# A four-layer graph network on one core: exponentials three calls behind their subtractions, four copies on another engine, a later transpose, an earlier load

## The chip, the core and the metric

The kernel runs on one core of one Trainium2 chip. The metric is the time of one execution on the device in microseconds (us). The time before is the median of three runs, 2242.59 us (2240.81 to 2247.57). The profile comes from one execution that took 2241.24 us.

## The reference, cut to what matters

There are N = 2708 nodes with 512 features each and a sparse symmetric 0/1 matrix `adj`. Four layers follow each other, and the result of each goes through a residual sum and a layer norm:

```python
# layer 0
pooled = a_norm @ x + x;  y = relu(pooled @ W + b)
# layer 1
dis = (deg + EPS) ** -0.5
y = (dis[:, None] * adj * dis[None, :]) @ x @ W.T + b
# layer 2: two attention layers, one behind the other
Wh, Ws = jnp.split(x @ W, 2, axis=-1)
a = softmax(Wh @ Ws.T, axis=-1) * adj
x = leaky_relu(a @ Wh + x)
# layer 3: 8 heads
y = adj @ (H @ W) + b
# behind each layer
x = layernorm(x + y)
```

## The kernel before, in words

**Tiling.** The nodes make 22 row blocks, 21 of 128 rows and one of 20 (`NB` = 22). Columns are cut into six chunks (`CH`): four of 512, one of 384, one of 276. `Fast.run` does layers 0 and 1 in steps of one chunk and one group of row blocks, then the two attention layers, then layer 3. The wrapper class `Ordered` ties each instruction to the one issued before it on its engine, so every engine runs its instructions in exactly the order in which the program issues them. This has two consequences for a reader: the order in the Python code is the order on the chip, engine by engine, and an instruction that waits holds all that stand behind it on its engine. All instructions of the trace carry the line of that wrapper, L71; they are told apart by the names of their tiles.

**Layers 0 and 1.** A product `acc` is the sum over row blocks of a mask `m` (a byte tile `at`, cast by ScalarE) times x, which is split in two parts: `xh` (ScalarE) and `xl`, the rest (VectorE), both from `halve`. In layer 1 both are scaled with `dis`. The last block of 20 rows is handled by `fold`: it lays four quarters of its x, 32 rows each, under each other (four copies on ScalarE), and in layer 1 does the same with the 32 values of `dis` (tile `dis_f`, four copies on VectorE). VectorE also does the reductions `feeds`, from which the lists of neighbours are made.

**An attention layer.** For each chunk, PE computes the 22 score tiles `s` (products `sp`, `spx`, `spy`; chunks 0 and 1, `SEVEN`, by a scheme with seven products in place of eight). VectorE keeps the greatest score of each column (`top`). Two steps of PE bring it into the form that is subtracted: `shift_rows` (transposes `tr_top`, reductions, copies to `wide`) and `shift_columns` (transposes `tr_mx`, a ScalarE copy to `shift`). Then the chunk is softened, one row tile after the other. A call v of `soften` issues

- the subtraction of tile v on VectorE (`s<-s,shift`),
- the exponential of the tile that is `apart` calls behind on ScalarE (`s<-s`),
- another `apart` calls behind: the sum (`sum<-sum,s`) and the mask product (`s<-s,a`) on VectorE, and the store of the tile by SyncE's queue, SP (`pairs<-s`).

`apart` is 2 for the chunks of `SEVEN` and 1 for the others. So a chunk of `SEVEN` takes 26 calls, the others 24; behind the last tile's mask product `softened` is set to `SOFT`, the sign that the chunk may be gathered. Then GpSimd (POOL) gathers rows of the stored tiles by lists of neighbours (`g<-pairs,givers`, `fetch`), at most 10 outstanding, and PE weighs them (`acc<-g`, `weigh`). The end of a block goes to `xr` and `r`, by `y<-r` to memory and turned round to the next layer's `xt` (layer 0), or through the layer norm into `made`, the x of layer 3 (layer 1).

**The order around the change.** The planner keeps a clock of its own, `self.clock`: each group of matmuls moves it on by its planned time (512 columns: 4 x 512 / 2400 us). `later` and `pending` hold work that is due at a time of this clock; `until(clock, fill)` issues weighing steps, or where none is ready steps of `fill`, till the clock is reached. In `layer`, a chunk's 22 score steps carry the softening of the chunk before: behind step 4 the old chunk is put on the list, and from step 5 on each step calls `soften_next` once or twice in turn (always twice where two chunks wait). That is 26 calls from step 5 to 21. Behind the last chunk's scores comes the tail:

```python
        self.until(self.clock + 3, fill)
        self.shift_rows(last)
        self.until(self.clock + 3, fill)
        self.shift_columns(last)

        while chunks[-3].to_fetch:
            if not self.weigh() and not next(fill, False):
                assert self.weigh(True)
        done = self.clock + (2 if ly.number == 0 else 4)
        while last.softened < SOFT:
            self.soften(last)
            done += 1.4
            self.until(done, fill)
```

The `fill` of attention layer 0 is `second`, the projection of attention layer 1: the product of the two weight halves (`mix`, four steps, each ended by a ScalarE copy to `mixed`), loads of the weights and of chunk 0's x (`load_xt`: four DMAs of SP, 1 MB for a full chunk, `xt<-t`), sums of quarters for the seven products (`t1x` to `t4x`, `s1mixed` to `s4w`, on VectorE: `sum_xt`, `sum_sides`), and for each chunk `project_steps`: products `wst` (ScalarE copies to `wst_sb`), products `z` and stores of `z_sb` (`pairs<-z_sb`). The x of chunk k + 1 is loaded ahead of the products of chunk k. The `fill` of attention layer 1 is `early`, the first twelve parts of layer 3's products, of four steps with eight matmuls each; its parts t = 0 and 1 call `need`, which forces the weighing of row blocks up to 11 and up to 15, whether their gathers have landed or not.

The functions that the diff touches, and what calls them:

Of the kernel before, what the change touches and what calls it, by code (L numbers as in the profile page):

```python
# [22 lines left out]
NB = 22  # L23
# [4 lines left out]
CH = [(0, 512), (512, 512), (1024, 512), (1536, 512), (2048, 384), (2432, 276)]  # L28
# [8 lines left out]
QUARTERS, QW = 4, P // 4  # L37
# [16 lines left out]
class Ordered:  # L54


    def __init__(self, tc):
        self.tc, self.last = tc, {}
        for name in ("tensor", "vector", "scalar", "gpsimd", "sync"):
            setattr(self, name, OrderedEngine(self, getattr(tc.nc, name)))  # L60
# [440 lines left out]
}  # L501
STREAMED = 4
FIRST_LANDS = 16
SOFT = NB + 2 * 2
ALONE = 18
SEVEN = [0, 1]
PROJECTED = [0, 1]
# [44 lines left out]
class Fast:  # L552
# [275 lines left out]
    def fold(self, ly, x, s):  # L828


        nc = self.nc
        f = self.page(f"fold{ly.number}")[:, :P]
        for d in range(DC):
            nc.scalar.copy(f[d * QW : (d + 1) * QW], x[:QW, bass.ts(d, P)])
        if ly.number == 1:
            t = self.small.tile([P, 1], FP, tag="dis_f", name="dis_f")
            for d in range(DC):
                nc.vector.tensor_copy(t[d * QW : (d + 1) * QW], s[:QW])
            s = t
        return f, s  # L840

# [741 lines left out]
class Chunk:  # L1583


    def __init__(self, ly, k):
        self.ly, self.k, self.cw = ly, k, CH[k][1]
        self.name = f"{ly.number}_{k}"
        self.blocks = blocks_of(k)
        self.s, self.masks, self.ends = {}, {}, []  # L1590
        self.half = self.cw // 2
        self.seven = k in SEVEN
        self.part, self.complete, self.ready, self.top = {}, [], [], None
        self.softened = 0
        self.masks_ahead = 2 if k < STREAMED else 5
        self.apart = 2 if self.seven else 1
        self.fetched, self.rden = [], None
        self.x, self.first = {}, {}
        self.rows = set()
        self.mv = None  # L1600

        self.to_weigh = []
        for q, (i, _, _) in enumerate(self.blocks):
            ts = lists_of(i)
            self.to_weigh += [(q, t, t is ts[0], t is ts[-1]) for t in ts]
        self.to_fetch = [(q, t) for q, ts, _, _ in self.to_weigh for t in ts]
        self.first_fetch = self.to_fetch[0]
# [11 lines left out]
class Attention:  # L1619
# [656 lines left out]
    def soften_next(self):  # L2276


        if self.to_soften:
            self.soften(self.to_soften[0])  # L2280
            if self.to_soften[0].softened == SOFT:
                self.to_soften.pop(0)

    def soften(self, ch):


        nc, v, cw = self.nc, ch.softened, ch.cw
        ch.softened += 1
        if v < NB:
            n = rows_of(v)  # L2290
            s = ch.s[v][:n, :cw]
            nc.vector.tensor_sub(s, s, ch.shift[:n, :cw])
        j = v - ch.apart
        if 0 <= j < NB:
            s = ch.s[j][: rows_of(j), :cw]
            nc.scalar.activation(s, s, AF.Exp)
        j -= ch.apart
        if j < 0:
            return
        if j == NB - 1:  # L2300
            ch.softened = SOFT
        if j == 0 and ch.k >= 2:
            while self.chunks[ch.k - 2].to_fetch:
                self.weigh(True)
        if j % DC == 0 and j + ch.masks_ahead * DC < NB:
            self.load_mask(ch, j // DC + ch.masks_ahead)
        n = rows_of(j)
        s = ch.s[j][:n, :cw]
        if j == 0:
            ch.sum = self.page(f"sum{ch.name}")  # L2310
            nc.vector.tensor_copy(ch.sum[:, :cw], s)
        else:
            nc.vector.tensor_add(ch.sum[:n, :cw], ch.sum[:n, :cw], s)
        nc.vector.tensor_mul(s, s, ch.masks.pop(j)[:n, :cw])
        to = ch.ly.pairs[ch.k % 2][j * P : j * P + n, :]
        if cw == BANK:
            nc.sync.dma_start(
                to[:, : 2 * PAIR].rearrange("j (r x) -> j r x", x=PAIR)[:, :, D:],
                ch.s[j][:n, :].rearrange("j (r x) -> j r x", x=2 * P),
            )  # L2320
            return
        for r in range(2):
            w = min(2 * P, cw - r * 2 * P)
            nc.sync.dma_start(
                to[:, r * PAIR + D : r * PAIR + D + w],
                ch.s[j][:n, r * 2 * P : r * 2 * P + w],
            )
# [50 lines left out]
    def fetch_ahead(self):  # L2378
        count = sum(len(c.fetched) for c in self.chunks)
        for c in self.chunks:  # L2380
            while c.to_fetch:
                if c.softened < SOFT or count >= self.AHEAD:
                    return
# [140 lines left out]
    def layer(self, ly, chunks, fill):  # L2524
        f = self.f
        self.chunks, self.made = chunks, {}
        for k, ch in enumerate(chunks):
            old = chunks[k - 1] if k else None
            following = chunks[k + 1] if k + 1 < len(chunks) else None

            n = -1
            for what in self.walk(ch):
                if what == "mid":
                    self.soften_next()
                    self.weigh()
                    continue
                n += 1
                if old and n < old.masks_ahead:
                    self.load_mask(old, n)
                if not following and n > NB - 1 - ch.masks_ahead:  # L2540
                    self.load_mask(ch, n - NB + ch.masks_ahead)
                if old and n < 2:
                    self.greatest(old, last=n == 1)
                many = 2 if len(self.to_soften) > 1 else 1 + n % 2
                for _ in range(0 if ch.seven else many):
                    self.soften_next()
                f.beat()
                if n == 14 and k:
                    f.packed(k - 1)
                if following and n == 15:  # L2550
                    self.load_moving(following)
                if following and following.seven and n == 18:
                    self.sum_moving(following)
                if not following and n in (5, 11, 19):
                    next(fill)
                if ch.seven and not following.seven and n >= 7 and n % 4 == 3:
                    self.restore(ly, n // 4 - 1)
                if not ch.seven and n == 1:
                    for i in sorted(ly.sums):
                        self.restore(ly, i)  # L2560
                self.greatest(ch)

                for _ in range(3):
                    if not self.weigh():
                        break
                if old and n == 2:
                    self.shift_rows(old)
                if old and n == 4:
                    self.shift_columns(old)
                    self.to_soften.append(old)  # L2570
        assert not self.to_soften
        last = chunks[-1]
        self.greatest(last, last=True)
        self.until(self.clock + 3, fill)
        self.shift_rows(last)
        self.until(self.clock + 3, fill)
        self.shift_columns(last)
# [9 lines that stand above are left out]
        while any(c.to_weigh for c in chunks):  # L2587
            if not self.weigh() and not next(fill, False):
                assert self.weigh(True)
        while self.pending:  # L2590
            if not next(fill, False):
                self.pending.pop(0)[1]()
        for _ in fill:
            pass
# [13 lines left out]
    def second(self, first):  # L2608

        ly = self.layers[1]  # L2610
        mixing = self.mix(1)
        next(mixing)
        yield True
        self.load_w(ly)
        yield True
        self.load_xt(ly, 0)
        yield True
        yield from mixing
        if ly.seven:
            self.sum_xt(ly, 0)  # L2620
            yield from self.sum_sides(ly)
        for k in range(len(CH)):
            if k + 1 == len(CH) - 1:
                while self.pending:
                    self.pending.pop(0)[1]()
                self.first_moving(first)
            if k + 1 < len(CH):
                self.load_xt(ly, k + 1)
            yield from self.project_steps(ly, k)


# [63 lines left out]
```

## Time and profile before

| | before |
|---|---|
| median of three runs | 2242.59 us (2240.81 to 2247.57) |
| the profiled execution | 2241.24 us |
| its span, first to last instruction | 2239.3 us |
| mean granted clock of TensorE | 0.993 |
| PE idle in the span | 36.4 us |
| ScalarE's wait for VectorE's subtractions (`s` for `s`) | 53.7 us in 44 waits, longest 7.9 |
| gathers by POOL | 510, mean 1051 ns |
| moved by DMA | 502.29 MB, mean 224 GB/s |

How to read it: a row of a timeline gives start, duration, engine, operation, output from inputs, and, in brackets, how long the engine stood idle before it and what released it. A table of waits gives, for one engine, total us, number of waits and the longest. A table of windows gives for each stretch its length, the busy time of each engine (and its instructions), the granted clock (1.00 is full speed), the DMA engines' share and the rate. PE is TensorE's matmul, PEld its weight load, DVE VectorE, ACT ScalarE, SP the queue of SyncE. A DMA share over 1.00 means that all 16 engines had something to move all the time.

### The profile page before, as it was taken

To read this page: it belongs to the slowest core of one execution; us is meant where nothing else is said; L and a number is where in the kernel's file an instruction comes from. 1 tells how busy PE (TensorE), PEld (TensorE's weight loads), DVE (VectorE), ACT (ScalarE), POOL (GpSimd) and SP (SyncE) were. 2 spreads that over 40 slices of the span, in tenths; PEclk is the share of its full clock that TensorE was granted. 3 is DMA by queue.
4 is the path that set the end of the run, shared out by engine and by line. 5 is a ranking of instruction groups with operands and counts; after the bars stand their busy time and mean duration, and the time that the engine had idled before them with its cause. 6 is when DMAs were issued, how large, how long until landed. Compare 5 with 4: busy or idle time off the path is not lost.

```text
span 2239.3 us, 29396 instructions
## 1 busy us (share of the span) xinstructions
PE 2202.9 (98%) x9652; PEld 1507.3 (67%) x9652; DVE 1590.5 (71%) x3346; ACT 771.8 (34%) x1683; POOL 718.0 (32%) x827
## 2 busy tenths in 40 slices
PE   9999999999999999999999999999999999899997
PEld 6777787889877887443555666787443555477896
DVE  6777888887887869856676733459868788625734
ACT  7444353333333234222332322234322334342121
POOL 2333440111000000556466442000466467543000
PEclk9999999999999999999999999999999999999999
DMA  9976761223467615889799899704889799974321
GB/s 349 284 214 170 197 189 47 89 79 104 148 260 284 236 36 158 282 289 325 247 358 357 301 398 358 282 24 149 268 289 338 256 346 352 338 215 134 106 75 42
DMA packets 273619, 502.29 MB, mean 224 GB/s; under 512 B 41646, under 2 KB 133478, under 8 KB 273456
## 3 DMA queue, kind: packets, MB, share of 16 engines
q1 hardware_dynamic: 204800, 285.36, 36.9%
q0 software_dynamic: 68656, 214.96, 29.2%
q8 instruction: 78, 1.28, 0.2%
q14 instruction: 85, 0.70, 0.1%
HBM read 314.37 MB, written 185.83 MB: 223 GB/s over the span
## 4 chain that ended last, share of the span: by engine, by line
PE 85%; DVE 7%; DMA 6%; SPq 1%; issue 1%; ACT 1%; POOL 0%; DVEq 0%; ACTq 0%
PE acc L71 33%; PE sp L71 21%; PE spx L71 6%; PE spy L71 5%; PE mm L71 4%; PE mmx L71 3%; PE mmy L71 2%; DMA pairs<-s 2%; DMA x<-x 2%; PE wst L71 2%; PE z_0x L71 2%; DVE s L71 1%; SPq L71 1%; PE z_0y L71 1%; PE z_1x L71 1%; DMA xt<-t 1%
## 5 line engine op out<-in xcount | busy, mean ns | idle before, releaser
L71 POOL DMA_INDIRECT g<-pairs,givers x510 | 536.0, 1051 | 806.6 <-DMA pairs<-s 224.2
L71 PE MATMUL acc<-m,xh 128*128 128x512 f32 (+4 forms) x1584 | 565.5, 378 | 7.9 <-ACT m L71 6.6
L71 PE MATMUL acc<-m,xl 128*128 128x512 f32 (+4 forms) x1584 | 550.5, 365 | 0.3 <-DVE xl L71 0.3
L71 PE MATMUL sp<-xs,wst_sb 128*128 128x512 f32 (+4 forms) x1440 | 512.3, 521 | 0.0
L71 PEld LDWEIGHTS sp<-xs,wst_sb 128*128 128x128 f32 (+1 forms) x1440 | 255.9, 185 | 245.8 <-issue 167.5
L71 PEld LDWEIGHTS acc<-m,xh 128*128 128x128 f32 (+1 forms) x1584 | 288.7, 188 | 68.6 <-issue 18.3
L71 PEld LDWEIGHTS acc<-m,xl 128*128 128x128 f32 (+1 forms) x1584 | 289.0, 189 | 43.1 <-issue 3.3
L71 PE MATMUL acc<-g 128*32 128x512 f32 (+1 forms) x1020 | 269.1, 607 | 3.3 <-DMA g<-pairs,givers 2.4
L71 ACT COPY s<-sp 128x512 f32<-128x512 f32 (+2 forms) x172 | 87.7, 511 | 455.2 <-PE sp L71 429.8
L71 ACT CAST m<-at 128x512 fp32r<-128x512 uint8 (+5 forms) x396 | 200.0, 566 | 63.9 <-DMA at<-mask 23.9
L71 DVE TENSOR_TENSOR sum<-sum,s 128x512 f32<-128x512 f32 (+4 forms) x252 | 157.2, 624 | 51.0 <-ACT s L71 50.6
L71 PEld LDWEIGHTS acc<-g 128*32 128x32 f32 (+1 forms) x1020 | 76.2, 135 | 146.1 <-issue 110.7
L71 DVE TENSOR_TENSOR s<-s,a 128x512 f32<-128x512 f32 (+3 forms) x264 | 165.9, 628 | 9.1
L71 DVE TENSOR_TENSOR top<-top,s 128x512 f32<-128x512 f32 (+3 forms) x240 | 149.2, 622 | 23.6 <-ACT s L71 21.6
L71 ACT ACTIVATE s<-s 128x512 f32<-128x512 f32 (+3 forms) x264 | 146.9, 579 | 53.8 <-DVE s L71 53.7
L71 DVE TENSOR_TENSOR s<-s,shift 128x512 f32<-128x512 f32 (+3 forms) x264 | 162.4, 620 | 2.3 <-ACT shift L71 2.3
L71 POOL DMA_DIRECT2D x<-o x44 | 25.5, 586 | 301.3 <-DVE o L71 257.3
L71 DVE SCALAR_TENSOR_TENSOR xr<-acc,rden,xr 128x512 f32<-128x512 f32 (+1 forms) x44 | 32.9, 747 | 99.9 <-PE acc L71 99.8
L71 PE MATMUL mm<-w,ht 128*128 128x512 f32 (+1 forms) x240 | 98.8, 594 | 0.0
L71 ACT ACTIVATE rs_t<-rs_v 128x4 f32<-128x4 f32 (+3 forms) x31 | 6.4, 205 | 264.9 <-DVE rs_v L71 264.9
L71 DVE SCALAR_TENSOR_TENSOR odd<-at 128x512 bf16<-128x512 f32 (+2 forms) x132 | 82.3, 624 | 9.2 <-DMA at<-in_adj_t 7.1
L71 POOL DMA_DIRECT2D mask<-some x72 | 43.3, 605 | 135.3 <-ACT some L71 127.2
(345 smaller groups left out, 2932.6 us busy)
## 6 DMA issues: line engine op xcount, KB each, us to landing
pairs<-z_sb SPq DMA_DIRECT2D x84, 768.0 KB
pairs<-s SPq DMA_DIRECT2D x168, 256.0 KB
at<-in_adj_t SPq DMA_DIRECT2D x84, 256.0 KB
xres<-x POOLq DMA_DIRECT2D x44, 256.0 KB, 4.9
x<-o POOLq DMA_DIRECT2D x43, 256.0 KB, 3.2
pairs<-s SPq DMA_DIRECT2D x84, 128.0 KB
a<-mask SPq DMA_DIRECT2D x40, 256.0 KB
x<-x SPq DMA_DIRECT2D x37, 256.0 KB
```

The costliest lines, as they stand in the source:

```text
L71: ins = call(*args, **kw)
```

## The change

- One distance `APART` = 3 takes the place of `apart`: the exponential is issued three calls behind its subtraction, and the sum, the mask product and the store one call behind the exponential. All chunks now take `SOFT` = 26 calls.
- The four copies of `dis` in `fold` go from VectorE to ScalarE.
- Before the last chunk's `shift_rows`, `until` runs 5 us of the planner's clock instead of 3.
- In `second`, chunk k + 1's x is loaded as before (the check of the last index now lies in `load_xt`, which returns when there is no such chunk or it is loaded already); in the step of k = 1, chunk 3's x is loaded as well, one step earlier than before.

```diff
 STREAMED = 4
 FIRST_LANDS = 16
-SOFT = NB + 2 * 2
+APART = 3
+SOFT = NB + APART + 1
...
             for d in range(DC):
-                nc.vector.tensor_copy(t[d * QW : (d + 1) * QW], s[:QW])
+                nc.scalar.copy(t[d * QW : (d + 1) * QW], s[:QW])
...
-        self.apart = 2 if self.seven else 1
...
-        j = v - ch.apart
+        j = v - APART
         if 0 <= j < NB:
             s = ch.s[j][: rows_of(j), :cw]
             nc.scalar.activation(s, s, AF.Exp)
-        j -= ch.apart
+        j -= 1
         if j < 0:
             return
...
         self.greatest(last, last=True)
-        self.until(self.clock + 3, fill)
+        self.until(self.clock + 5, fill)
         self.shift_rows(last)
...
-            if k + 1 < len(CH):
-                self.load_xt(ly, k + 1)
+            self.load_xt(ly, k + 1)
+            if 0 < k < STREAMED - 2:
+                self.load_xt(ly, k + 2)
             yield from self.project_steps(ly, k)
```

## The prediction

> **What bounds the kernel.** I read the page first, then PE's waits, then busy time stage by stage, and last the order of the instructions around each of PE's stalls.
>
> ```profile
> span 2239.3 us, 29396 instructions
> PE 2202.9 (98%) x9652; PEld 1507.3 (67%) x9652; DVE 1590.5 (71%) x3346; ACT 771.8 (34%) x1683; POOL 718.0 (32%) x827
> PE 85%; DVE 7%; DMA 6%; SPq 1%; issue 1%; ACT 1%; POOL 0%; DVEq 0%; ACTq 0%
> ```
>
> TensorE is busy 98% of the span and carries 85% of the chain. The change takes no matmul away, so all it can win lies in PE's 36.4 us of idle time (2239.3 − 2202.9) and in time at a reduced clock. PE's waits say who causes them (total, times, longest):
>
> ```profile
> PE acc L71 <- ACT m L71: 6.6, 3, 3.9
> PE wst_0x L71 <- ACT wst_sb L71: 3.9, 1, 3.9
> PE wst_0x L71 <- DMA xt<-t: 2.0, 2, 1.2
> PE tr_top L71 <- DVE top L71: 1.7, 1, 1.7
> ```
>
> Elsewhere, from 600 to 1205 and from 1320 to 1885 us, PE is never idle for long, so nothing that the change does to exponentials there can win time; it could only lose. Windows around the stalls (start:end, length, busy time of PE, PEld, DVE, ACT, POOL; then PE's clock, DMA share, GB/s) show the second cost, half clock after a stall:
>
> ```profile
> 342.00:345.20 3.20, 3.20 (x10) 2.42 (x9) 3.20 (x4) 1.24 (x3) 0.00 (x0) 0.50 0.00 0
> ```
> ```profile
> 1248.00:1253.00 5.00, 5.00 (x12) 4.01 (x13) 4.86 (x12) 2.32 (x7) 0.95 (x1) 0.50 1.04 391
> 1253.00:1266.00 13.00, 13.00 (x70) 11.33 (x69) 12.55 (x33) 8.28 (x23) 0.00 (x0) 0.99 0.62 206
> 1312.00:1319.00 7.00, 3.83 (x15) 2.15 (x14) 1.47 (x4) 1.56 (x4) 3.77 (x4) 1.00 1.04 409
> 1319.00:1375.00 56.00, 55.91 (x248) 39.05 (x248) 23.42 (x56) 16.13 (x40) 16.39 (x17) 1.00 1.04 397
> ```
> ```profile
> 1899.60:1928.70 29.10, 26.12 (x60) 6.30 (x59) 7.34 (x14) 5.45 (x10) 22.09 (x24) 0.94 1.03 408
> 1947.70:1952.90 5.20, 4.82 (x11) 3.40 (x12) 4.83 (x11) 4.17 (x9) 3.77 (x6) 0.50 0.84 244
> ```
>
> So there are three places: 338, 1248 and 1947 us.
>
> **Place 1, start of layer 1: copies of dis.** ScalarE, then VectorE (start, duration, what; idle before and its releaser):
>
> ```profile
> 332.06 1.22 ACT L71 COPY fold<-o 32x128 f32<-32x128 f32 x4
> 339.67 0.40 ACT L71 ACTIVATE xh<-fold,dis_f 128x128 fp32r<-128x128 f32 x1 [6.39 <-DVE dis_f L71]
> ```
> ```profile
> 333.23 4.47 DVE L71 TENSOR_REDUCE feeds<-at 128x64 bf16<-128x2048 uint8 x2
> 338.94 0.61 DVE L71 COPY dis_f<-dis 32x1 f32<-32x1 f32 x4
> ```
>
> ScalarE waits 6.39 us for four copies of 32 values that stand on VectorE behind 4.47 us of reductions and 1.39 of xl; behind its xh stand the mask casts m, and PE waits 1.91 us for them (338.56 to 340.63). The change puts the copies right behind the four fold copies on the idle ScalarE. The trace has no ScalarE copy of 32x1: between 0.20 us (its 128x4 activation, rs_t) and 0.30 (1.22/4 for 32x128) each. I take 0.30, the row of the same operation: 1.2 us for four, from 333.3 to 334.5, xh to 334.9, two casts (1.12) to 336.0, ahead of PE's 338.56. What is late next is xl on VectorE: without the 0.61 us of copies it starts at 338.94 and ends 0.35 later, 339.3, where PE wants it about 338.9. The stall shrinks from 1.91 to 0.4: 1.5 us. At half clock a matmul comes every 0.43 us instead of 0.23; for seven matmuls that is 1.4 us, and it goes with the stall. Place 1: **2.9 us**, at least 1.0 if VectorE, 80 to 90% busy here, gives part back at its next products, at most 3.3.
>
> On that clock: 0.50 follows stalls of 1.91, 3.86 and 3.92 us; none follows the 1.69 us before tr_top. The Trainium skill (TensorE: Matmul & The Clock Gate, Part 1: The HAM clock gate) lets the clock drop only after an idle window of about 3.4 us. By that rule the 1.91 us stall would cost no clock and place 1 be worth 1.5. The row of 342.0 to 345.2 disagrees, and I follow the row.
>
> **Place 2, end of attention layer 0: exponentials and maxima.** Here the last chunk's softening (subtract, exponential, sum, mask) is interleaved with layer 1's weight products.
>
> ```profile
> 1234.74 1.08 ACT L71 ACTIVATE s<-s 128x276 f32<-128x276 f32 x3
> 1245.77 0.43 ACT L71 ACTIVATE s<-s 128x276 f32<-128x276 f32 x1 [7.88 <-DVE s L71]
> 1247.55 0.38 ACT L71 COPY wst_sb<-wst_0x 128x256 f32<-128x256 f32 x1
> ```
> ```profile
> 1235.21 0.45 DVE L71 TENSOR_TENSOR sum<-sum,s 128x276 f32<-128x276 f32 x1 [2.82 <-ACT s L71]
> 1245.30 0.44 DVE L71 TENSOR_TENSOR s<-s,shift 128x276 f32<-128x276 f32 x1
> ```
>
> With a lag of one, each exponential needs the subtraction of the call just before it. VectorE first loses 4.00 and 2.82 us waiting for exponentials behind copies of mixed on ScalarE, then does 8.05 us of operand sums (1237.25 to 1245.30); the exponential whose subtraction stands behind these waits 7.88 us, and the wst_sb copies queued behind it on ScalarE hold PE for 3.86 us at 1247.98 (another 0.53 at 1240.4 is for s1mixed, among the sums). Then come three groups of four matmuls at 1.70 us instead of 0.865: 2.5 us. Loss in all: 0.53 + 3.86 + 2.5 = 6.9. With a lag of three the subtractions run two calls further ahead, ScalarE has arguments while VectorE sums, and VectorE does not wait for ScalarE; the three idle times of before (4.00, 2.82, 7.88) have no cause left. The later tr_top (5 us on the planner's clock instead of 3) only takes another step of fill or weighing ahead; what it delays, the softening, has cover: its end (1275.6) moves by about −2 to +2.
>
> Not all of 6.9 stays won. From 1266 DMA share is 1.00 to 1.04, and at 1312 to 1319 PE waits 3.2 us (1.21 + 0.78 + 0.26 + 0.93) for chunk 2's xt, issued by SP at 1292.4 behind stores of z_sb that waited for their totals. These totals come some 4 to 7 us earlier too, so xt(2) lands earlier, perhaps less than PE arrives. I take **5.0 us**; lowest 1 (the wait grows by almost all), highest 6.9.
>
> The x loads: xt(3) goes out with chunk 1's step instead of chunk 2's, past y<-r, quarter, xr and pairs<-z_sb on SP. Now it is issued at 1331.65 (5.95 us for four), VectorE's first sum on it waits 9.35 us, PE uses it at 1352.1 without waiting. The megabyte moves ahead of the stores behind it, about 2.6 us at 400 GB/s; between the ends of −2.6 and +3.2 (all of the xt waits) I take 0, the row where PE does not wait.
>
> **Place 3, end of attention layer 1.** At 1899.6 to 1928.7 weighing is forced and bound by gathers: POOL issues one in 1.26 us, PE is busy 26.12 of 29.10. Then eight or nine softening calls come in a burst ahead of the next group's xh and xl:
>
> ```profile
> 1946.22 0.43 ACT L71 ACTIVATE s<-s 128x276 f32<-128x276 f32 x1 [0.76 <-DVE s L71]
> 1946.56 0.61 ACT L71 ACTIVATE xh<-x 128x512 fp32r<-128x512 f32 x1
> ```
>
> PE waits 3.92 for m and 0.35 for xl, then runs at half clock to 1952.9 (ten pitches, 2.0): 6.3. The change acts three ways. Exponentials stop waiting 0.76 each. Softening calls are spread 1.4 planned us apart among the products, since the forced stretch, reached later, comes ahead of the first call and not among them: the burst goes, **+6.3**. Against that, stores of chunks 3 and 4 come one call later, so their gathers do: one score step (1.86 us) for the first list, two for later ones, **−3.3** (between −1 and −9, if a POOL-bound stretch starts later still). The 1.69 us before tr_top lie inside that stretch and are worth 0. Place 3: **+3**, from −3 to +6.3.
>
> In the body the longer lag keeps a row tile in use for a call or so more. The first two chunks already softened in 26 calls; their exponential moves one call later and the sum stays. The others go from 24 calls to 26, at one or two a score step (1.86 us), so their stores end a step later. PE's queue of ready work covers it: 0, and at worst one 6.3 us stall as at 1947.
>
> **Sum.** 2.9 + 5.0 + 3 = 10.9 us. The profiled execution took 2241.24 (span plus 1.94), 1.35 under the median. 2242.59 − 10.9 = **2231.7**. All high ends (16.5) give 2226, all low ones (−1) 2243.6.
>
> **Rivals.** *A, given back downstream:* xt(2) and the gathers bound their stages, place 2 leaves 1 to 2, place 3 about 0: 2242.59 − 2.9 − 1.5 = 2238. For it: DMA shares over 1.00 on both sides; against: 0.62 at 1253 to 1266, room for the loads. *B, the change does not do it:* exponentials still stand behind PSUM copies on ScalarE, the waits only shift: 2240. Against: the three idle times each name a subtraction one call old. *C, slower, at place 3:* spread softening overloads VectorE. A call is 1.19 us of it, 1.5 us apart; a pair of groups (14.6 us of PE) holds 9.7 calls, 11.5 us, and four xl, 2.5: 14.0. If its other work exceeds 0.6 us there, every later group's xl is late, as once now, for 6.3: three groups cost 18.9. With places 1 and 2 won (7.9), today's burst gone (6.3) and the gathers' 3.3 lost: 2242.59 − 7.9 + 18.9 − 6.3 + 3.3 = 2251; it decides from the second late group on. For: that narrow margin; against: from 1953 to 1963 VectorE is 97% busy with such calls and PE never waits.
>
> **Chances.** Forecast 0.62, A 0.18, B 0.05, C 0.15. About 0.3%, 6.7 us, can be told from no change: A and B fall within it, so faster 0.62, same 0.23, slower 0.15. The range goes from 2225 (all high ends, and another us) to 2247, leaving out most of C.
>
> **What would show it.** Step 1: no idle of ScalarE for dis_f, clock 1.00 at 342. Step 2: no 7.88 wait, no half clock near 1250; the xt(2) wait under 4. Step 3: no PE wait for m after the forced stretch, which ends 3 us later against the scores' end. A wait for pairs<-s or g longer than now, or half clock in layer 3's products, would make the forecast wrong.

## The result, and the profile after

The kernel after takes 2235.46 us (median of 11 runs, 2234.20 to 2239.84); the kernel before, beside it, 2242.49 (11 runs). The ratio is 0.9974, 95% interval 0.9964 to 0.9983: 7.0 us between the medians, 3.8 to 8.1 by the interval. The profiled execution took 2235.33 us, its span is 2233.6, 5.7 less than before. Page of the kernel after:

```profile
span 2233.6 us, 29413 instructions
PE 2196.9 (98%) x9652; PEld 1504.0 (67%) x9652; DVE 1590.0 (71%) x3342; ACT 771.7 (35%) x1687; POOL 711.8 (32%) x827
```

The same matmuls take 6.0 us less busy time, mainly since fewer of them run at half clock (mean granted clock 0.995 instead of 0.993); PE's idle time is 36.7 us, as much as before (36.4). So one set of stalls was exchanged for another. PE's waits in the kernel after:

```profile
PE acc L71 <- ACT m L71: 8.9, 3, 7.8
PE acc L71 <- DVE xl L71: 4.1, 1, 4.1
PE tr_top L71 <- DVE top L71: 1.7, 1, 1.7
PE wst_0x L71 <- DMA xt<-t: 0.4, 1, 0.4
```

The 3.9 for wst_sb is gone, xt costs 1.5 in all instead of 3.2, but the longest wait for m has grown from 3.9 to 7.8, and one of 4.1 for xl is new. Where the time went is read from the start of the same instruction in both traces. Four marks do: the first scores of attention layer 0 with the shifted operand (`sp<-xs`), the first scores of attention layer 1, its last tr_top, its last `den`.

| start of, us | before | after | won up to here | won in the stretch |
|---|---|---|---|---|
| scores, attention layer 0 | 808.21 | 805.17 | 3.0 | 3.0 (place 1) |
| scores, attention layer 1 | 1419.98 | 1406.62 | 13.4 | 10.3 (place 2) |
| last tr_top | 1891.63 | 1891.45 | 0.2 | −13.2 (place 3) |
| last den | 2008.30 | 2002.58 | 5.7 | 5.5 (place 3) |

**Place 1** in the kernel after, on ScalarE, VectorE and in a window:

```profile
333.47 0.79 ACT L71 COPY dis_f<-dis 32x1 f32<-32x1 f32 x4
334.30 0.40 ACT L71 ACTIVATE xh<-fold,dis_f 128x128 fp32r<-128x128 f32 x1
```
```profile
339.12 0.33 DVE L71 SCALAR_TENSOR_TENSOR xl<-fold,dis_f,xh 128x128 fp32r<-128x128 f32 x1
```
```profile
338.50:342.00 3.50, 3.50 (x20) 2.30 (x20) 3.50 (x5) 0.59 (x1) 0.00 (x0) 1.00 0.26 75
```

Nothing waits in front of xh any more; PE is busy all 3.50 us at clock 1.00, where it had 1.59 of 3.50 and half clock behind it.

**Place 2**, windows of the kernel after:

```profile
1240.00:1256.00 16.00, 16.00 (x88) 13.88 (x81) 15.18 (x37) 10.46 (x29) 6.50 (x6) 1.00 0.88 301
1300.00:1305.00 5.00, 4.47 (x20) 1.90 (x19) 1.09 (x3) 1.22 (x3) 0.00 (x0) 1.00 1.05 392
```

The weight products run through at full clock, and at chunk 2's xt PE loses 0.4 us instead of 3.2, although it comes there at 1303.0 instead of 1312.7. SP's queue issues the x of chunks 2 and 3 in one go, ahead of the next stores of z_sb (1309.32), and PE uses chunk 3's x at 1337.4 without waiting:

```profile
1289.61 13.98 SPq L71 DMA_DIRECT2D xt<-t  x8
```

**Place 3** is where the gain was given back. VectorE, ScalarE and PE of the kernel after, then windows:

```profile
1871.80 0.69 DVE L71 TENSOR_TENSOR r<-r,x 128x512 f32<-128x512 f32 x1 [10.26 <-DMA x<-x]
```
```profile
1873.91 0.52 ACT L71 ACTIVATE s<-s 128x384 f32<-128x384 f32 x1 [12.07 <-DVE s L71]
```
```profile
1877.05 0.79 PE L71 MATMUL acc<-m,xh 128*128 128x512 f32 x1 [7.81 <-ACT m L71]
1881.94 0.80 PE L71 MATMUL acc<-m,xl 128*128 128x512 f32 x1 [4.11 <-DVE xl L71]
```
```profile
1870.00:1877.00 7.00, 0.00 (x0) 0.00 (x0) 5.06 (x11) 2.08 (x5) 5.18 (x6) 0.73 1.02 377
1877.00:1887.20 10.20, 6.05 (x11) 3.69 (x12) 9.99 (x21) 8.76 (x18) 0.00 (x0) 0.51 0.94 301
1930.00:1960.00 30.00, 30.00 (x132) 24.37 (x131) 19.02 (x44) 15.94 (x34) 11.35 (x14) 1.00 0.82 271
```

Read the first four lines downwards: VectorE stands 10.26 us for the residual x of chunk 3's first block; the subtractions stand behind it, so the exponentials on ScalarE; behind those stand xh and m of layer 3's first products, which are issued as a fill step among the last scores; and PE waits 7.81, then 4.11 for xl, and runs at half clock. The last window shows what was won behind it: the old stall at 1947 is gone. Why x was late is on SP's queue. Before:

```profile
1856.37 0.43 SPq L71 DMA_DIRECT2D x<-x  x1
1860.58 3.03 SPq L71 DMA_DIRECT2D x<-x  x4
```

After:

```profile
1852.73 4.28 SPq L71 DMA_DIRECT2D x<-x  x5
1860.72 16.57 SPq L71 DMA_DIRECT2D pairs<-s  x14
```

The single x at 1856.37 is that residual, ahead of layer 3's first ten loads (two mask tiles and eight x of 256 KB, 2.6 MB). After the change it is the last of the five at 1852.73, behind the ten; it was issued by 1857.0 and landed 14.8 us later. Chunk 3's weighing begins one score step later, and at just that step (number 11) the program issues the ten loads. Stores changed sides too: before, chunk 4's row tiles 0 to 8 go out ahead of the ten loads, after only 0 to 6.

### The profile page after: what moved, and what is told of

The parts are those of the page before. It is cut to its first block, busy times and chain, and to the rows that moved or that the text cites. A ratio compares the mean times of both kernels' runs of the same rounds, so it can differ in the third digit from the quotient of the medians.

```text
span 2233.6 us, 29413 instructions
## 1 busy us (share of the span) xinstructions
PE 2196.9 (98%) x9652; PEld 1504.0 (67%) x9652; DVE 1590.0 (71%) x3342; ACT 771.7 (35%) x1687; POOL 711.8 (32%) x827
## 4 chain that ended last, share of the span: by engine, by line
PE 87%; DMA 7%; DVE 3%; ACT 1%; SPq 1%; issue 1%; POOL 0%; DVEq 0%; ACTq 0%; POOLq 0%
PE acc L71 33%; PE sp L71 22%; PE spx L71 6%; PE spy L71 5%; PE mm L71 3%; PE mmx L71 3%; PE mmy L71 2%; DMA at<-in_adj_t 2%; PE z_0x L71 2%; PE wst L71 1%; PE wst_0x L71 1%; PE z_0y L71 1%; PE wst_1x L71 1%; PE z_1x L71 1%; DMA xt<-t 1%; DMA x<-in_x 1%
## 5 line engine op out<-in xcount | busy, mean ns | idle before, releaser
L71 POOL DMA_INDIRECT g<-pairs,givers x510 | 530.4, 1040 | 805.6 <-DMA pairs<-s 240.9
```

The source lines that it names most:

```text
L71: ins = call(*args, **kw)
```

## The experiments

Theory A: the loss at place 3 is this order on SP. Theory B: it is the lag itself, as work of VectorE and ScalarE. Theory C: the DMA engines are full there, and the same bytes come late in any order. For place 2 the question was which part won the 10.3. The stretches of each profiled execution (us between the marks), and the ratio to the kernel before in the same series:

| kernel | to scores of layer 1 | to last tr_top | to last den | ratio, 95% interval |
|---|---|---|---|---|
| before | 611.8 | 471.7 | 116.7 | 1 |
| after | 601.5 | 484.8 | 111.1 | 0.9974, 0.9964 to 0.9983 |
| e1 loads at step 12 | 601.4 | 479.4 | 113.3 | 0.9956, 0.9938 to 0.9975 |
| e2 before, loads at step 9 | 612.7 | 478.3 | 112.0 | 1.0016, 1.0005 to 1.0027 |
| e3 lag alone | 609.5 | 484.1 | 115.8 | 1.0048, 1.0031 to 1.0066 |
| e4 early x alone | 614.8 | 471.7 | 118.2 | 1.0003, 0.9989 to 1.0016 |
| e5 loads at step 8 | 604.0 | 477.7 | 112.3 | 0.9956, 0.9941 to 0.9970 |
| e6 loads on another queue | 602.4 | 477.0 | 113.4 | 0.9962, 0.9949 to 0.9975 |
| e7 without the later tr_top | 602.6 | 484.5 | 115.6 | 1.0000, 0.9988 to 1.0011 |
| e8 without the early x | 612.7 | 482.9 | 112.0 | 1.0030, 1.0017 to 1.0043 |
| e9 lag in layer 0 only | 621.1 | 476.1 | 121.5 | 0.9966, 0.9941 to 0.9991 |
| e10 and in the last chunk | 613.6 | 479.8 | 121.8 | 0.9975, 0.9950 to 1.0000 |
| e11 without the lag | 619.4 | 482.5 | 118.5 | 0.9969, 0.9939 to 0.9999 |
| e12 as e9 | 623.3 | 475.3 | 119.0 | 0.9955, 0.9926 to 0.9984 |

The last four ran where the kernel before itself took 2268 to 2271 us, so their stretches can't be set beside the others; their ratios and the order of their stalls can.

**The order turned round in the kernel after (e1).**

```diff
-                if not following and n in (5, 11, 19):
+                if not following and n in (5, 11 + ly.number, 19):
```

> The kernel after, with one number changed: the third-last fill step of attention layer 1, which issues layer 3's first ten loads (2.6 MB), comes at score step 12 instead of 11, so that the residual x of the first block of chunk 3 is again ahead of them on SP, as in the kernel before. Theory A (the new stall comes from that order: the residual queues behind 2.6 MB, holds VectorE 10.26 us, and with it exponentials, xh and m): VectorE's wait for x is under 2 us, PE's waits of 7.81 and 4.11 and the half clock behind them are gone, the time is 2222 to 2228, that is 8 to 13 below the kernel after. Theory B (the longer lag itself makes VectorE and ScalarE late there): the stall stays above 8 us of PE, 2234 to 2237. Theory C (the DMA engines are full, and whatever is loaded then comes late): the stall moves to another load, 3 to 8 us of it stay, 2229 to 2234.

Measured: 2232.88 us. VectorE's wait of 10.26 is gone, as A says (this r<-r,x starts at 1862.26 without idle time), and so are PE's 7.81 and 4.11. But only 5.4 us come back by the last tr_top, and 3.3 by the last den: other waits are behind it. PE waits 2.30 for xl, 2.29 for a ScalarE copy, 4.09 before tr_top. ScalarE and VectorE in this kernel:

```profile
1876.44 0.39 ACT L71 COPY s<-sp 128x276 f32<-128x276 f32 x1 [5.12 <-DMA pairs<-s]
```
```profile
1884.53 0.69 DVE L71 TENSOR_TENSOR r<-r,x 128x512 f32<-128x512 f32 x1 [4.38 <-DMA x<-x]
```

A copy of scores needs a tile whose store has not landed. These stores still stand behind the ten loads (tiles 0 to 7 are ahead of them here, 0 to 8 in the kernel before). The second row is the residual of chunk 3's second block: SP issues it at 1877.79, behind twelve of these stores, and VectorE waits for it again. So A named the first wait rightly. But it expected no wait for x above 2 us, and it had the price wrong: some of the loss moves on to later transfers, as C has it, and the time lies in C's range.

**The order turned round in the kernel before (e2).**

```diff
-                if not following and n in (5, 11, 19):
+                if not following and n in (5, 11 - 2 * ly.number, 19):
```

> The kernel before, with the same fill step at score step 9 instead of 11, so that layer 3's first ten loads go out ahead of the residual x of chunk 3's first block; the lag of the exponentials stays 1. Theory A (order of these loads): VectorE waits 3 to 10 us for the residual x near 1868, PE waits 2 to 12 us with half clock behind it, 2245 to 2254. Theory B (the lag): no new wait of PE, 2241 to 2244.

Measured: 2244.24 us, under A's range, and the stall is there without any longer lag. VectorE and PE of this kernel:

```profile
1875.83 0.69 DVE L71 TENSOR_TENSOR r<-r,x 128x512 f32<-128x512 f32 x1 [6.03 <-DMA x<-x]
```
```profile
1890.14 0.79 PE L71 MATMUL acc<-m,xh 128*128 128x512 f32 x1 [4.08 <-ACT m L71]
```

B does not explain this. The stretch to the last tr_top is 6.6 us longer; 4.7 of it come back behind it.

**Each part of the change alone (e3, e4).** The lag alone is the diff's first, third and fourth piece; the early x alone its last.

> The kernel before with the new lag alone (three calls to the exponential, one to the sum, 26 calls for all chunks). If the lag is what won place 2, the start of attention layer 1's scores moves 6 to 10 us earlier (it moved 13.4 with everything, 3.0 of it from place 1), and the new stall of about 13 us near 1870, less the 5.5 us won behind it, is there as well: 2239 to 2243 in all. Rival: the later transpose or the earlier load won place 2; then the lag alone wins under 3 there and the time is 2246 to 2250.

Measured: 2252.24 us, slower than either expectation. The stall at 1248 and its half clock are gone (from 1235 to 1260 PE is busy 25.00 us at clock 1.00), yet the stretch to the scores of layer 1 is only 2.2 us shorter: PE then waits 4.29, 0.58 and 0.26 us for chunk 3's xt. At place 3, up to the last den, it loses 11.6, with 9.20 us of VectorE's wait for x.

> The kernel before with chunk 3's x loaded one chunk earlier, and nothing else. Theory: the wait for chunk 2's x (3.2 us at 1312 to 1319) stays, since it was issued in front of it as before; 2241 to 2244. Rival 1: the extra megabyte delays stores and chunk 2's x shares the engines with it: 2.6 us more, 2245. Rival 2: it takes away waits: 2239 to 2240.

Measured: 2243.77 us, no difference; the wait for chunk 2's xt stays (1.69 and 0.77 in its longest parts), as the theory had it.

**The ten loads elsewhere (e5, e6).** In e5 they go out at score step 8; in e6 ScalarE's DMA queue issues them.

```diff
-                if not following and n in (5, 11, 19):
+                if not following and n in (5, 8 if ly.number else 11, 19):
```

> The kernel after, with layer 3's first ten loads (2.6 MB) at score step 8 instead of 11: they still go out ahead of the residual x and of the stores of chunk 4's row tiles 2 and later, but 5.6 us earlier, so they should have drained before those are due. Theory A2 (both holds near 1870, that of the residual and that of score tiles whose stores have not landed, come from queueing behind this block of loads): VectorE's wait for x falls from 10.26 to under 5 us, PE loses 0 to 6 us instead of 13 before the last tr_top, 2222 to 2230. Theory C (the DMA engines are simply full from 1850 on, and the same bytes are late wherever they stand): the loss stays 9 to 13 us, 2232 to 2237.

> The kernel after, with layer 3's first ten loads issued from ScalarE's DMA queue instead of SP's, at the same place of the program: the residual x and the stores no longer stand behind them in one queue, but the bytes and the engines that move them are the same. Theory A2 (order in SP's queue): VectorE's wait for the residual is under 4 us, ScalarE waits under 2 for a stored tile, 2222 to 2230. Theory C (engines full): the waits stay above 6 us, 2232 to 2238. A side cost can be up to 3 us of ScalarE for issuing ten loads.

```diff
-        self.nc.sync.dma_start(at[:, : j1 - j0, :], self.k.masks[k][:, j0:j1, :])
+        queue = self.nc.scalar if ly.number == 3 and k == 0 and g < 2 else self.nc.sync
+        queue.dma_start(at[:, : j1 - j0, :], self.k.masks[k][:, j0:j1, :])
...
             queue = self.nc.gpsimd if ly.number == 1 else self.nc.sync
+            if ly.number == 3 and j < GROUPS[2][0]:
+                queue = self.nc.scalar
```

Measured: 2232.06 and 2234.30 us. VectorE in e5:

```profile
1868.89 0.69 DVE L71 TENSOR_TENSOR r<-r,x 128x512 f32<-128x512 f32 x1 [1.87 <-DMA x<-x]
```

This residual was issued at 1861.43, 13.8 us behind the last of the ten loads, and the DMA engines were full on its way (share 1.04 from 1861 to 1869). VectorE waits 1.87 us for it and not 10.26, so on this wait the order decides, as A has it, and not the full engines of C. In e6 VectorE does not wait for the residual at all, and no wait of ScalarE for a store is left among the last scores. But e6 parts the queue from the engines less well than was meant: its residual goes out at 1858.81, 5.9 us behind the last of the ten (1852.92), and the share is then 0.94 to 0.99 (1858 to 1866). Whether the common queue matters, or only the bytes issued just before, stays open. Both stretches to the last tr_top are 7 to 8 us shorter than in the kernel after. But both times are above A's range (the profiled execution of e6 took 2231.5) and inside C's: A does not explain the rest of the loss. In e6 ScalarE stands 12.80 us in its own loads, which costs PE 2.38, and tr_top waits 4.10; in e5 xl is still 4.08 late. The intervals of e1, e5 and e6 overlap that of the kernel after, so none is shown to be faster than it.

**The change without one part (e7, e8).**

> The kernel after with 3 us instead of 5 before the last tr_top, all else changed. If the later tr_top is what made the lag pay at place 2 (the lag alone moved the start of the next scores only 2.2 us, everything together 10.3), place 2 wins 2 to 5 here: 2239 to 2245. If it is the earlier load of x (rival), place 2 keeps its 10: 2233 to 2237.

> The kernel after without the earlier load of chunk 3's x. If the later tr_top is what made the lag pay, place 2 keeps 8 to 10 us: 2233 to 2238. If the load is (rival), place 2 wins only 2 to 5: 2239 to 2245.

Measured: 2243.65 and 2249.47 us, the first inside the range of my expectation, the second above both ranges. At place 2, however, my expectation fell and the rival held: without the later tr_top the stretch is 602.6, as after; without the early x it is 612.7, and nothing is won. Queue of SP and PE in e8:

```profile
1309.39 17.25 SPq L71 DMA_DIRECT2D pairs<-z_sb  x8
1326.70 8.03 SPq L71 DMA_DIRECT2D xt<-t  x4
```
```profile
1346.70 1.19 PE L71 MATMUL wst_0x<-xt,mixed 128*128 128x256 f32 x2 [7.22 <-DMA xt<-t]
```

Chunk 3's xt stands behind eight stores that SP issues over 17.25 us, and PE, which now comes earlier, waits for it. The later tr_top pays at place 3: from layer 1's first scores to the last den it is 600.1 without it and 596.0 with it. (With the lag alone, also without it, 600.0.) In e7 the last tr_top waits 3.08 us and half clock follows (0.50 from 1896.9 to 1900.3); in the kernel after it waits 1.73 at clock 1.00. By the ratios, 1.0000 against 0.9974, the later tr_top is worth some 6 us in all.

**The lag only where it wins (e9 to e12).** The old lags are kept in attention layer 1 (e9, e12), in all but its last chunk (e10), or everywhere (e11).

```diff
+        new = ly.number == 0
+        self.apart = (APART, 1) if new else (2, 2) if self.seven else (1, 1)
...
-        j = v - APART
+        j = v - ch.apart[0]
...
-        j -= 1
+        j -= ch.apart[1]
         if j < 0:
```

In e10 the first line reads `new = ly.number == 0 or k == len(CH) - 1`; e11 is the kernel before with the other three parts.

> The kernel after, with the old lags (2 and 2, or 1 and 1) in attention layer 1 and the new one in attention layer 0 only. SP's order near 1860 is that of the kernel before: residual first, nine row tiles stored ahead of layer 3's loads. Theory A2 (the loss at place 3 is the order that the lag shifts there): places 1 and 2 keep their 13.4 us, place 3 is as in the kernel before, with its stall of 6.3 after the forced stretch: 2227 to 2231. Rival (place 3 loses for another part of the change, the later tr_top, or because PE arrives earlier): 2234 to 2238.

> As the previous one, with the new lag in the last chunk of attention layer 1 as well, which is softened behind the scores. If that chunk's longer lag is what takes away PE's 6.3 us behind the forced stretch, 2221 to 2226. If the stall went because the lag of chunks 3 and 4 moved the forced stretch ahead of the softening calls (rival, and the way the prediction put it), it stays here: 2227 to 2231.

> The kernel after with the old lags everywhere: copies on ScalarE, later tr_top and earlier load of x remain. If the lag is needed at place 2, PE's wait near 1248 and the half clock stay and the scores of attention layer 1 start 0 to 6 us earlier than in the kernel before, 3 of it from place 1: 2237 to 2243. If the later tr_top and the load do it without the lag (rival), the start is 10 to 13 us earlier and place 3 is as before: 2229 to 2233.

> The same kernel as in the run before last series (new lag in attention layer 0 only), because there the kernel before itself took 2271 us instead of 2242 and weight products and gathers waited longer than in any other run. Theory A2 as before, where the kernel before is at 2240 to 2244: the scores of attention layer 1 start 13 us earlier than in the kernel before, from there to the last den as in the kernel before (588 us), 2227 to 2231 in all. Rival (the loss at place 3 is not the lag's): that stretch takes 593 to 597, 2234 to 2238.

Measured: 2260.22, 2263.82 and 2259.83 us beside 2270.82, and 2259.00 beside 2268.29. No expected time applies, and the ratios overlap that of the kernel after, so whether e9 beats it stays open. The stalls answer the questions. In none of the four, all with the old lag in chunks 3 and 4 of attention layer 1, does VectorE wait for a residual x among the last scores. In the kernels with the new lag there and the ten loads in their old place (after, e3, e7, e8) it waits 10.26, 9.20, 9.69 and 8.27 us. In e9:

```profile
1860.00:1890.00 30.00, 29.88 (x126) 17.71 (x125) 29.34 (x63) 10.72 (x25) 22.15 (x20) 1.00 0.95 333
```

The stall behind the forced stretch is there in e9 (5.44 for m) and e12 (2.37). In e10 it is not gone (1.55 and 3.02 with half clock), which speaks for the prediction's reason, the lag of chunks 3 and 4, and against the last chunk's own; one profile there is no proof. In e11 a stall of place 2 stays without the lag:

```profile
1250.78 2.08 PE L71 MATMUL wst_0x<-t3x,s3mixed 128*128 128x256 f32 x4 [2.71 <-ACT wst_sb L71]
```

But with the lag PE loses as much there in this series (3.28 us at 1242.43 in e9, 3.99 at 1260.50 in e12), so it does not tell whether the lag is needed at place 2. The kernel before, e3 and e4 do: the 3.86 us stall goes with the lag alone and stays with the early x alone.

## Why the prediction was right, and where it was not

The forecast was a gain of 10.9 us; 7.0 were measured, on the forecast side and inside the range. That the sum came so near is luck: two terms were off by 5.3 and 10.6 us, in opposite directions.

- **Place 1** held in its mechanism, with luck in its size: 2.9 forecast, 3.0 measured. The ScalarE copies took 0.20 us each, not 0.30. In this execution xl was not late, so PE had no stall at all; in the nine other kernels with these copies PE waits 0.38 to 0.69 us for xl, as forecast (0.4). And half clock, 1.4 of the 2.9, followed the old stall in the kernel before and in e3, but not in e2 and e4, where the stall was 2.40 and 2.39. Where it does not follow, the change is worth some 1.7 us (an estimate, 2.39 − 0.69).
- **Place 2**, 5.0 forecast, 10.3 measured, above the highest value given (6.9). The removed stall was as described: all three idle times are gone, and e3 shows that the lag alone does this. The step that failed is the term for chunk 3's x, taken as 0 because PE did not wait for it before. In that row PE came to this load at 1352.1; without the stall it comes at 1342.7 (e3) or 1339.5 (e8) and waits. With the lag in place the early load is worth 11.2 us (612.7 in e8 against 601.5), without it nothing (614.8 in e4 against 611.8). The ends given for this term (−2.6 and +3.2) were also left out of the sums of all high and all low ends, and the DMA share was not 1.00 or more from 1266 on: it was 0.92 up to 1280 and 1.03 to 1.04 behind that. Rival A, that place 2 is given back downstream, is what e3 and e8 did; the early load is why the whole change did not.
- **Place 3**, +3 forecast, −7.6 measured, below the lowest value given (−3). The burst's 6.3 went as forecast. The gathers' −3.3 came as −1.7 (the first product behind the forced stretch starts 37.1 us after the last tr_top before, 38.8 after), and 5.5 were won behind the last tr_top. The step that failed is "so their stores end a step later. PE's queue of ready work covers it: 0". The delay was followed to the gathers, not past SP's queue: the residual x and two more row tiles' stores fell behind layer 3's ten loads, and the stretch up to the last tr_top became 13.2 us longer (some 2 of it, an estimate from the 5 and 3 us of planned time, are work that the later tr_top moves ahead of it). e1, e2 and e5 show the order to be the cause of the 10.26 us wait, and e6 agrees. e1, e5 and e6 bring back 5 to 8 of the 13.2; what makes up the rest, VectorE's backlog before xl and tr_top, the next block's residual (4.38 in e1) or more, is not settled.
- **The later tr_top**, taken as work merely moved ahead, is worth some 4 us at place 3 (e7), where it shortens its own wait and spares the half clock behind it.
- **Rival C** (VectorE overloaded by spread softening in layer 3's products) did not come: PE is busy 30.00 of 30 us from 1930 to 1960.

## What to carry to other kernels

A delay of one step that an engine's slack covers can still reorder a queue, as at place 3: list, for each step that moves, which DMAs on the same queue it passes, and who waits in program order behind the one that lands last. And a load that nobody waits for is priced against the arrival time after the change: at place 2 removing the stall was worth 2.2 us alone (e3), loading the next operand early nothing alone (e4), and both together 9.2 (e7).

## What the runs showed of the hardware that was not expected

A 256 KB load issued right behind 2.6 MB in one queue landed 14.8 us later (after); issued 13.8 us behind the last of the same 2.6 MB, it landed 7.5 us later (e5), in both at a DMA share of 1.04. Half clock followed PE stalls of 1.91 (before), 2.38 (e6) and 2.71 us (e11), but not those of 1.73 (after), 2.05 (e8, clock 1.00 from 1901.5 to 1905), 2.40 (e2, clock 1.00 from 343 to 348) and 3.28 (e9, clock 1.00 from 1242.4 to 1247.4). No single length separates them, and the Trainium skill's idle window of about 3.4 us (TensorE: Matmul & The Clock Gate, Part 1: The HAM clock gate) does not either. Apart from the last, at the kernel's end, every stretch at half clock in these traces lasted 3.4 us or a multiple of it: 342.0 to 345.4 and 1246.5 to 1253.3 before, 1873.3 to 1886.9 after.
